# A four-layer graph network on one core: where neighbour rows are summed, and who adds the bias, the residual and the row sums

## The chip, the cores and the metric

The kernel runs on one core of a Trainium2 chip. That core has a matrix engine (PE, with its weight loads listed as PEld), a vector engine (DVE), a scalar engine (ACT), a general engine (POOL), a queue engine that issues plain transfers (SP), and 16 DMA engines. The engines run side by side, each takes its own instructions strictly in order, and they wait for one another through semaphores. The metric is the device time of one execution in microseconds (us): the median of three runs before the change is 1075.28 us (1071.92 to 1076.54).

## The reference, cut to what matters

There are 3327 nodes with 512 features each, and an adjacency matrix of 3327 x 3327 that is nearly empty (a node has about four neighbours). Four layers follow one another, all of the form x = x + layer(relu(layernorm(x))):

```
layer 0:  relu( self + (sum of neighbours' rows) / degree + bias )   self and neighbour weights folded beforehand
layer 1:  8 heads; softmax over the neighbours of leaky_relu(src + dst); weighted sum of the neighbours' rows
layer 2:  4 heads, the same, then elu
layer 3:  1 head, the same; weighted sum of the normalised inputs, then one 512 x 512 product with W
```

Every layer needs, for each node, the rows of its neighbours as the layer before left them. So no layer may gather a row before that row has been written.

## The kernel before, in words

**Preparation.** The kernel reads the whole adjacency matrix, and DVE finds the columns that hold a one. It makes a list of at most 16 neighbours per node (16 is `SLOTS`), sorts the nodes by falling degree, and cuts the sorted nodes into 26 chunks of 128. After the sort, slot s of a chunk is needed only by the nodes that have more than s neighbours. `ROWS` says how many sorted nodes may have a slot s; `CAPS` is the same in chunks, and `slots_of` turns it round: chunk 0 has 14 slots, chunk 1 has 8, chunks 2 and 3 have 7, chunks 4 to 6 have 6, 7 to 10 have 5, 11 to 15 have 4, 16 to 20 have 3, 21 to 23 have 2, 24 and 25 have 1. That is 117 slots in all. Alongside, PE multiplies the normalised input with the two folded weights of layer 0. The neighbour part goes to a table in DRAM. The own part is copied by ACT (`keep_y`, L1373) beside the input row, and POOL scatters both, with the list of neighbours, to the node's sorted place (`scatter`, L1435, one indirect transfer per chunk, 26 in all). One transfer (`back`, L1451) then brings the lists of all sorted nodes back into on-chip memory (`srec`), and DVE takes the reciprocal degrees from it (`degrees`, L1505 and L1506).

**The layers.** A layer goes through its chunks in units of one or two, in the order that `ORDERS` lists. For each slot of a chunk POOL issues one indirect transfer (`gather`, L1562) that brings 128 rows, or fewer where `held` says that fewer are needed, into one place of a ring of 33 places. A place is written again only when its readers are done. In layer 0 DVE notes the neighbours' sorted places (L1862), PE adds the first slots into PSUM by products with the identity matrix (`sum_on_pe`, L1593), DVE divides by the degree and adds the own part (L1871), adds the bias (L1879), adds the last `ON_DVE` slots one by one (L1887), and takes the relu and adds the input (L1895). In layers 1 and 2 DVE makes the scores and weights of a unit (L1941 to L1978), multiplies the rows in the ring by the weights (L2110; the first `ON_ACT` slots on ACT, L2096, one instruction per head), PE sums the slots, and in layer 1 DVE adds some of them (L2138). Then the result is added to the running x (L2148, L2172 and L2178). In layer 3 ACT and DVE weigh and add the rows (L2028, L2030), PE turns the sum (L2046), multiplies the residual by the identity (L2058) and the sum by W (L2060) into the same PSUM place, ACT copies it out (L2067), and POOL scatters it to the node's original row of the output (L2072).

**From one layer to the next.** `project` takes the mean and variance of the new rows on DVE (`bn_stats`, L1649 and L1650), guesses the reciprocal root on ACT (L822, L824) and refines it on DVE in four small operations per unit (L831 to L836), normalises on ACT (L1676), turns on PE (L1694), copies on ACT with column sums (L1705), multiplies by the next layer's weights on PE (L1780, eight products per chunk), copies on ACT (L1803 to L1806) and stores the rows to the next layer's table through SP (L1822). A switch `SUMMED` would take the mean from a row sum that the update leaves behind and the variance from a square on ACT; it is off for all layers. A layer's first gather waits for all stores of the layer before; a memset on POOL (`mark`, L2194) carries that wait.

**What sets the order.** `Plan` is a list scheduler that runs while the kernel is built. Each piece of work is given an engine, a cost in us and the pieces it follows; the plan replays them and emits the instructions in the order it finds. So the instruction order on every engine comes from the plan's costs, and at run time the engines keep to it.

Of the kernel before, what the change touches and what calls it, by code (L numbers as in the profile page):

```python
# [13 lines left out]
ALU = mybir.AluOpType  # L14
# [4 lines left out]
P = 128  # L19
# [7 lines left out]
def general_path(  # L27
# [519 lines left out]
    def l3_finish(pc, i, o):  # L547
# [16 lines left out]
ROWS = (3328, 3072, 2592, 1984, 1344, 832, 448, 224, 128, 64, 32, 32, 32, 32, 0, 0)  # L564
# [8 lines left out]
    0: {S: min(S // 2, 5) for S in range(1, SLOTS + 1)},  # L573
    1: {S: min(S // 2, 5) for S in range(1, SLOTS + 1)},
    2: {S: 0 for S in range(1, SLOTS + 1)},
# [4 lines left out]
        (24,), (12, 21), (11,), (6,), (18,), (17,), (15,), (4,), (3,), (20,), (5, 9), (22,), (10, 19), (1,),  # L580
        (2,), (14,), (0,), (23,), (8,), (13, 16), (7,), (25,),
    ),
    1: (
        (18, 21), (22, 24), (15,), (5,), (10, 20), (2,), (17,), (12, 23), (19,), (4,), (9, 14), (7,), (11, 16),
        (8, 13), (6,), (1,), (0,), (3,), (25,),
    ),
    2: (
        (18, 23), (19, 24), (16,), (20,), (6, 11), (10, 14), (7, 12), (5, 13), (9,), (1,), (21, 22), (4,), (0,),
        (8,), (2,), (3,), (15,), (17,), (25,),
    ),  # L590
    3: (
        (0,), (7,), (17,), (15, 20), (25,), (11,), (3,), (23,), (1, 5), (24,), (4, 14), (16,), (12, 22), (8,),
        (9,), (10,), (18,), (2,), (13,), (19,), (21,), (6,),
# [4 lines left out]
    1: {S: min(S // 3, 1) for S in range(1, SLOTS + 1)},  # L598
    2: {S: S // 5 for S in range(1, SLOTS + 1)},
}  # L600

SUMMED = {1: False, 2: False, 3: False}
# [90 lines left out]
def gnn_stack_kernel(  # L693
# [41 lines left out]
    with ExitStack() as st:  # L735
# [116 lines left out]
        with tc.tile_pool(name="p0", bufs=1) as pa, tc.tile_pool(name="p0p", bufs=2, space=PSUM) as pp:  # L852
# [444 lines left out]
            for p0 in range(0, NK, 2):  # L1297
# [25 lines left out]
                for j, i in enumerate(unit):  # L1323
# [51 lines left out]
                    own_done[i] = put("act", 0.62, late_rank, keep_y, (), [y], give=("py",))  # L1375
# [74 lines left out]
            def back():  # L1450
                ins = nc.sync.dma_start(srec_f, own.rearrange("(k p) w -> p k w", p=P)[:, :, 2 * D :])  # L1451
                for other in scattered:
                    tc.add_manual_dep(
                        ins.ins,
                        other.ins.name,
                        mybir.DependencyInfo(mybir.DependencyClass.Sync, mybir.DependencyReason.DATA),
                        reason="every row is read",
                    )
# [57 lines left out]
        with tc.tile_pool(name="run", bufs=1, reuse_waits="tile") as pr, tc.tile_pool(  # L1516
# [28 lines left out]
            def gather(layer, i, rank, barrier):  # L1545
# [8 lines left out]
                for s in range(S):  # L1554
# [16 lines left out]
                    landed.append(plan.add("dma", 0.95 * held(i, s) / P, rank, None, [issue], lag=1.3))  # L1571
                return ring[:, r0 : r0 + S, :], landed, last

            def runs_of(i, lo, hi, most=SLOTS):
# [7 lines left out]
                return out  # L1582

# [262 lines left out]
            for number, unit in enumerate(ORDERS[0]):  # L1846
                rank = (0, number)
                updated = []
                for j, i in enumerate(unit):
# [15 lines left out]
                    left = S - ON_DVE[0][S]  # L1865
                    summed = sum_on_pe(key, g, list(range(left)), [[o] for o in landed], rank)
# [9 lines left out]

                    def emit(key=key):
                        acc = tiles["acc", key]
                        nc.vector.tensor_tensor(acc, acc, biasf, ALU.add)  # L1879

                    done = plan.add("dve", 0.7, rank, emit, [done])
                    for s in range(left, S):

                        def emit(i=i, key=key, g=g, s=s):
                            m = held(i, s)
                            acc = tiles["acc", key][:m, :]
                            nc.vector.scalar_tensor_tensor(  # L1887
                                acc, g[:m, s, :D], rdeg[:m, i : i + 1], acc, ALU.mult, ALU.add
                            )

                        done = plan.add("dve", 0.7, rank, emit, [done, landed[s]])
                        last.append(done)
# [18 lines left out]
            def attend(layer, number, unit, barrier):  # L1911
# [80 lines left out]
                for j, i in enumerate(unit):  # L1992
# [56 lines left out]
                    if layer == 3:  # L2049
# [16 lines left out]
                        def emit(key=key):  # L2066
                            nc.scalar.copy(new("t", key, [P, WIDE])[:, :D], tiles["pw", key][:, 0, :])  # L2067
# [192 lines left out]
```

## Time and profile before

| what | value |
|---|---|
| three runs | 1071.92, 1075.28, 1076.54 us |
| profiled execution: span from the first to the last instruction | 1230.0 us (the page gives no other time of this execution) |
| busy time over the span: PE, DVE, ACT, POOL | 901.8, 726.6, 518.2, 610.1 us |
| preparation, up to the first gather | 0 to 278 us |
| layer 0, 1, 2, 3 | 278 to 514, 514 to 759, 759 to 998, 998 to 1230 us |
| mean granted clock of TensorE | 0.855 |

The profiled execution is 154.7 us longer than the median run, or 1.144 times. So a sum made on the profile is about the profiled execution, and has to be carried over to the runs. The stage borders are read from the `mark` memsets on POOL (514.21, 759.46 and 998.45 us) and from the first gather (278.18 us). Busy time per stage is more useful here than the total, because each layer waits for the one before it: a layer is as long as its most loaded engine needs, plus the time in which that engine has nothing to do at the start and at the end. "Idle before" in the groups of instructions is the waiting time of an engine just before such an instruction, and costs nothing where that engine is not the bottleneck.

### The profile page before, as it was taken

What the parts mean: (1) busy time and instruction counts of PE and PEld (TensorE: products, weight loads), DVE (VectorE), ACT (ScalarE), POOL (GpSimd) and SP (SyncE); (2) the same over time, 40 slices, a digit from 0 to 9 for tenths busy, and PEclk for the clock granted to TensorE, in tenths of its full rate; (3) what the DMA queues carried; (4) which work ended last, traced back from release to release, by engine and by line L of the source; (5) the groups of instructions that cost most, each with busy time, mean ns of one, the idle gap of its engine ahead of it and who ended that gap; (6) DMA issues with size and microseconds to landing.
All of it is one profiled execution on the core that took longest, in us unless ns stands there. A gap on an engine that the chain in (4) does not pass through costs nothing. (4 is left out here: it accounts for less than half of the span.)

```text
span 1230.0 us, 11605 instructions
## 1 busy us (share of the span) xinstructions
PE 901.8 (73%) x2853; PEld 510.4 (41%) x2853; DVE 726.6 (59%) x1848; ACT 518.2 (42%) x1700; POOL 610.1 (50%) x719
## 2 busy tenths in 40 slices
PE   7599999854098889752979796539979832948865
PEld 4244444322075656531647464214435421423322
DVE  6499989204176557453869784628894815534441
ACT  4488886210043433422656553316554621312221
POOL 1064246717655550175757511766883236675661
PEclk9899999977599899966989889659896956978987
DMA  9999894958587772265666521665754345575561
GB/s 352 338 364 338 294 306 146 317 203 286 172 268 252 247 249 89 76 195 149 198 183 178 154 79 55 189 187 150 209 169 129 91 121 149 168 206 160 163 186 59
DMA packets 89910, 240.49 MB, mean 196 GB/s; under 512 B 24933, under 2 KB 26477, under 8 KB 89834
## 3 DMA queue, kind: packets, MB, share of 16 engines
q0 software_dynamic: 41600, 137.72, 38.1%
q1 hardware_dynamic: 48234, 101.96, 23.3%
q8 instruction: 24, 0.39, 0.1%
q14 instruction: 52, 0.43, 0.1%
HBM read 190.35 MB, written 49.27 MB: 195 GB/s over the span
## 5 line engine op out<-in xcount | busy, mean ns | idle before, releaser
L1562 POOL DMA_INDIRECT ring<-table,nbr x351 | 368.5, 1050 | 185.5 <-issue 80.9
L1593 PE MATMUL acc<-ring,ident 128*128 128x512 f32 (+1 forms) x494 | 266.6, 676 | 66.8 <-DVE ring L2110 24.3
L1780 PE MATMUL pw<-w,hT 128*128 128x264 f32 (+1 forms) x832 | 197.3, 394 | 18.3 <-ACT hT L1705 13.6
L1780 PEld LDWEIGHTS pw<-w,hT 128*128 128x128 f32 x832 | 161.2, 195 | 60.9 <-ACT hT L1705 20.5
L1593 PEld LDWEIGHTS acc<-ring,ident 128*128 128x128 f32 (+1 forms) x494 | 98.7, 215 | 175.1 <-issue 107.5
L1562 POOL DMA_INDIRECT ring<-table,srec x117 | 110.1, 941 | 77.8 <-issue 31.5
L2110 DVE TENSOR_TENSOR ring<-ring,w 128x2048 f32<-128x2048 f32 (+7 forms) x76 | 114.3, 1531 | 4.7 <-DVE w L1978 3.0
L2060 PE MATMUL pw<-w,hT 128*128 128x512 f32 x208 | 101.7, 634 | 13.3 <-ACT hT L2052 11.0
L1209 DVE FIND_INDEX8 fidx<-one_i,ai 128x8 uint32<-128x832 int32 x104 | 104.2, 1018 | 0.0
L1349 PE MATMUL pz_n<-wf,hT_n 128*128 128x512 f32 x208 | 95.2, 609 | 10.9 <-ACT hT_n L1342 8.4
L1705 ACT ACTIVATE hT<-pt 128x128 f32<-128x128 f32 (+1 forms) x312 | 81.8, 292 | 39.7 <-PE pt L1694 18.5
L1217 ACT ACTIVATE junk<-ai 128x1664 int8<-128x1664 int32 (+1 forms) x52 | 82.7, 1590 | 32.6 <-DMA ai<-in_adj_dram 32.2
L1694 PE MATMUL pt<-ident,h 128*128 128x128 f32 x208 | 36.5, 312 | 75.9 <-ACT h L1676 73.4
L1349 PE MATMUL py_n<-wf,hT_n 128*128 128x512 f32 x208 | 91.9, 592 | 0.0
L1803 ACT COPY t<-pw 128x512 f32<-128x512 f32 (+1 forms) x54 | 30.6, 566 | 134.0 <-PE pw L1780 43.9
L1941 DVE TENSOR_TENSOR e<-ring,fs 128x24 f32<-128x24 f32 (+25 forms) x96 | 15.2, 172 | 120.2 <-DMA ring<-table,nbr 102.0
L2060 PEld LDWEIGHTS pw<-w,hT 128*128 128x128 f32 x208 | 42.3, 207 | 73.2 <-issue 51.3
L1705 ACT ACTIVATION_READ_ACCUMULATOR hT<-pt 128x1 f32 x312 | 69.5, 223 | 0.0
L1694 PEld LDWEIGHTS pt<-ident,h 128*128 128x128 f32 x208 | 28.1, 160 | 96.3 <-ACT h L1676 81.6
L2194 POOL MEMSET mark<- 1x1 f32 x3 | 0.3, 88 | 132.7 <-DMA table<-t 132.7
L1349 PEld LDWEIGHTS pz_n<-wf,hT_n 128*128 128x128 f32 x208 | 39.8, 195 | 62.8 <-issue 49.4
L2046 PE MATMUL pt<-ident,y 128*128 128x128 f32 x96 | 16.4, 312 | 67.4 <-issue 56.8
(185 smaller groups left out, 1319.7 us busy)
## 6 DMA issues: line engine op xcount, KB each, us to landing
ai<-in_adj_dram SPq DMA_DIRECT2D x25, 832.0 KB
ai<-in_adj_dram SPq DMA_DIRECT2D x25, 831.5 KB
table<-t SPq DMA_DIRECT2D x52, 258.0 KB
xy<-own SPq DMA_DIRECT2D x26, 512.0 KB
table<-t SPq DMA_DIRECT2D x26, 260.0 KB
table<-zt_n SPq DMA_DIRECT2D x26, 256.0 KB
ring<-table,nbr POOLq DMA_INDIRECT x351
later<-in_x_dram SPq DMA_DIRECT2D x15, 256.0 KB
```

The source lines that it names most:

```text
L1209: nc.vector.max_index(fidx[:, i, qq * 8 : (qq + 1) * 8], one_i, ai[:, q * QW : min(cols, (q + 1) * QW)])
L1217: nc.scalar.activation(junk[:, :cols], tiles["ai", key][:, :cols], AF.Square, accum_out=sq[:, i, hf : hf + 1])
L1349: nc.tensor.matmul(pz, tiles["hT", key][:, c, :], wf[s][:, c, :], start=(c == 0), stop=(c == DC - 1))
L1562: nc.gpsimd.indirect_dma_start(out=ring[:m, r0 + s, : width[layer]], out_offset=None, in_=table[layer], in_offset=bass.IndirectOffsetOnAxi ...
L1593: nc.tensor.matmul(acc, ident[:m, :], g[:m, s, :D], start=(k == 0), stop=(k == len(slots) - 1))
L1694: nc.tensor.transpose(pt[:, c, :], h[:, c * P : (c + 1) * P], ident)
L1705: nc.scalar.activation(hT[:, c, :n], pt[:, c, :n], AF.Copy, accum_out=hsum[layer][:, i, c : c + 1])
L1780: nc.tensor.matmul(pw[:, b, :w], tiles["hT", key][:, c, :], wsb[layer][:, c, b, :w], start=(c == 0), stop=(c == DC - 1),)
L1803: nc.scalar.copy(t[:, :D].rearrange("p (b f) -> p b f", b=2)[:, lo:hi, :], pw[:, lo:hi, :HD])
L2046: nc.tensor.transpose(pt[:, c, :], tiles["y", key][:, c * P : (c + 1) * P], ident)
L2060: nc.tensor.matmul(pw[:, 0, :], tiles["hT", key][:, c, :], w3[:, c, :], start=False, stop=(c == DC - 1))
L2110: nc.vector.tensor_tensor(v, v, box["w"][:m, j, lo:hi, :].unsqueeze(3).to_broadcast([m, hi - lo, H, O]), ALU.mult,)
```

## The change

- Gathers always bring whole slots of 128 rows: `ROWS` is rounded up to multiples of 128. The number of slots stays 117.
- In layers 0, 1 and 2 a chunk's slots are summed either all on PE or all on DVE, by one `tensor_reduce` that reads the slots of a feature one after another (a step of 520 words in the ring) and then goes to the next feature. `ON_DVE` now lists the chunks: 18 in layer 0 (82 slots), 11 in layer 1 (65 slots), 2 in layer 2 (9 slots). The one-by-one additions on DVE are gone.
- The bias of layer 0 is added on POOL in the preparation, chunk by chunk, right after `keep_y`; DVE's addition in layer 0 is gone.
- `back` brings the lists in 26 transfers, one per chunk in layer 0's order, in place of one.
- `ON_ACT` is given per chunk: 15 slots in layer 1 (21 before), 33 in layer 2 (12 before).
- `SUMMED` is on for layer 2: the update of layer 1 leaves row sums, and ACT squares.
- In layer 3 DVE adds the residual while it reads the product; PE's identity product and ACT's copy are gone.
- Other orders in all four layers (19, 17, 17 and 21 units, in place of 22, 19, 19 and 22), and the ring starts at its first place in each layer.

```diff
-ROWS = (3328, 3072, 2592, 1984, 1344, 832, 448, 224, 128, 64, 32, 32, 32, 32, 0, 0)
+ROWS = (3328, 3072, 2688, 2048, 1408, 896, 512, 256, 128, 128, 128, 128, 128, 128, 0, 0)
 ON_DVE = {
-    0: {S: min(S // 2, 5) for S in range(1, SLOTS + 1)},
-    1: {S: min(S // 2, 5) for S in range(1, SLOTS + 1)},
-    2: {S: 0 for S in range(1, SLOTS + 1)},
+    0: frozenset((0, 2, 4, 5, 7, 9, 10, 11, 12, 13, 15, 17, 18, 19, 20, 21, 22, 23,)),
+    1: frozenset((0, 1, 3, 4, 5, 7, 8, 9, 12, 19, 22,)),
+    2: frozenset((2, 22,)),
 }
 ORDERS = {
     0: (
-        (24,), (12, 21), (11,), (6,), (18,), (17,), (15,), (4,), (3,), (20,), (5, 9), (22,), (10, 19), (1,),
-        (2,), (14,), (0,), (23,), (8,), (13, 16), (7,), (25,),
+        (22,), (24, 14), (13,), (17, 19), (23,), (18, 20), (3,), (15,), (21, 16), (8,), (12,), (2,), (11, 10),
+        (0, 5), (1,), (4, 7), (6,), (9,), (25,),
...
     1: (
-        (18, 21), (22, 24), (15,), (5,), (10, 20), (2,), (17,), (12, 23), (19,), (4,), (9, 14), (7,), (11, 16),
-        (8, 13), (6,), (1,), (0,), (3,), (25,),
+        (24,), (22,), (10,), (21, 20), (19,), (5, 17), (16,), (12,), (15, 7), (2, 3), (13, 9), (6, 14),
+        (4, 11), (23, 8), (1, 18), (0,), (25,),
...
     2: (
-        (18, 23), (19, 24), (16,), (20,), (6, 11), (10, 14), (7, 12), (5, 13), (9,), (1,), (21, 22), (4,), (0,),
-        (8,), (2,), (3,), (15,), (17,), (25,),
+        (24, 22), (16,), (23, 18), (19, 8), (13, 17), (21, 15), (4,), (12, 6), (10, 7), (1,), (14, 20),
+        (11, 9), (5,), (3,), (0,), (2,), (25,),
...
     3: (
-        (0,), (7,), (17,), (15, 20), (25,), (11,), (3,), (23,), (1, 5), (24,), (4, 14), (16,), (12, 22), (8,),
-        (9,), (10,), (18,), (2,), (13,), (19,), (21,), (6,),
+        (2,), (7, 4), (14,), (6, 12), (0,), (1, 3), (22,), (23,), (13,), (5,), (10,), (18, 21), (8,), (24,),
+        (9,), (11,), (25, 15), (19,), (16,), (17,), (20,),
...
 ON_ACT = {
-    1: {S: min(S // 3, 1) for S in range(1, SLOTS + 1)},
-    2: {S: S // 5 for S in range(1, SLOTS + 1)},
+    1: (1, 2, 1, 0, 2, 1, 2, 1, 0, 1, 0, 0, 0, 0, 0, 0, 1, 1, 1, 0, 0, 1, 0, 0, 0, 0),
+    2: (5, 3, 2, 2, 2, 1, 1, 3, 0, 0, 2, 3, 1, 2, 0, 1, 2, 1, 0, 1, 0, 0, 0, 1, 0, 0),
 }
-SUMMED = {1: False, 2: False, 3: False}
+SUMMED = {1: False, 2: True, 3: False}
...
-                    own_done[i] = put("act", 0.62, late_rank, keep_y, (), [y], give=("py",))
+                    o = put("act", 0.62, late_rank, keep_y, (), [y], give=("py",))
+                    def add_bias(i=i):
+                        own = node(i)[:, D : 2 * D]
+                        nc.gpsimd.tensor_tensor(own, own, biasf, ALU.add)
+                    own_done[i] = put("pool", 1.28, late_rank, add_bias, (), [o, whole])
...
-                ins = nc.sync.dma_start(srec_f, own.rearrange("(k p) w -> p k w", p=P)[:, :, 2 * D :])
+                for k in (k for unit in ORDERS[0] for k in unit):
+                    ins = nc.sync.dma_start(srec_f[:, k, :], own[k * P : (k + 1) * P, 2 * D :])
...
+            def sum_on_dve(key, g, S, needs, rank):
+                def emit():
+                    nc.vector.tensor_reduce(
+                        new("acc", key, [P, D], pp), g[:, :S, :D].rearrange("p s d -> p d s"), AX.X, ALU.add
+                    )
+                return [plan.add("dve", 0.1 + 0.535 * S, rank, emit, needs, take=("acc",))]
...
-                            nc.tensor.matmul(pw[:, 0, :], ident, xres[:, i, :], start=True, stop=False)
...
-                            nc.scalar.copy(new("t", key, [P, WIDE])[:, :D], tiles["pw", key][:, 0, :])
+                            nc.vector.tensor_tensor(
+                                new("t", key, [P, WIDE])[:, :D], tiles["pw", key][:, 0, :], xres[:, i, :], ALU.add
+                            )
```

## The prediction

> **What bounds the kernel now.** I read the busy times by stage first, because a layer cannot gather before the layer before it has stored, so each stage has a bound of its own.
>
> ```profile
> core 0: us, PE busy (x) PEld busy (x) DVE busy (x) ACT busy (x) POOL busy (x), PEclk, DMA share, GB/s
> 0.00:278.00 278.00, 234.03 (x639) 110.37 (x639) 187.22 (x520) 163.33 (x263) 104.95 (x222) 0.95 0.83 295
> 278.00:514.00 236.00, 173.87 (x651) 118.85 (x652) 130.56 (x305) 77.36 (x353) 110.13 (x117) 0.88 0.65 209
> 514.00:759.00 245.00, 180.97 (x652) 121.84 (x651) 165.93 (x397) 119.27 (x539) 124.02 (x118) 0.85 0.51 149
> 759.00:998.00 239.00, 172.54 (x550) 93.81 (x548) 151.47 (x374) 110.60 (x449) 134.12 (x118) 0.78 0.52 153
> 998.00:1230.00 232.00, 140.40 (x364) 65.50 (x364) 91.37 (x252) 47.59 (x96) 136.86 (x144) 0.79 0.53 156
> ```
>
> PE is the most loaded engine in layers 0, 1 and 2, with DVE 15 us behind in layer 1. PE's time without work is 62.1, 64.0 and 66.5 us there. In layer 3 POOL leads: an issue lasts 0.95 us with 0.30 us between, so 143 issues take 179 of its 232 us.
>
> The waits say where a stage loses time:
>
> ```profile
> POOL mark L2194 <- DMA table<-t: 132.7, 3, 56.1
> ...
> POOL out_dram L2072 <- ACT t L2067: 37.1, 10, 5.9
> ```
>
> POOL ends its gathers long before a layer ends (132.7 us over three borders), so layers 0 to 2 are not set by the gathers but by the work that lags behind them. In layer 3 POOL itself waits for finished outputs. Next, the groups of instructions that the edits touch, shapes apart:
>
> ```profile
> L1593 PE MATMUL acc<-ring,ident 128*128 128x512 f32 x472 | 254.0, 675 | 66.7 <-DVE ring L2110 24.3 <-issue 22.6 <-DMA ring<-table,srec 15.3
> ...
> L1649 DVE BATCH_NORM_STATS2 st<-xres 128x6 f32<-128x512 f32 x78 | 53.7, 689 | 2.0
> ...
> L1887 DVE SCALAR_TENSOR_TENSOR acc<-ring,rdeg,acc 128x512 f32<-128x512 f32 x39 | 29.4, 755 | 1.2
> ...
> L2138 DVE TENSOR_TENSOR acc<-ring,acc 128x512 f32<-128x512 f32 x39 | 27.0, 693 | 18.5 <-PE acc L1593 17.0 <-issue 0.9
> ...
> L1879 DVE TENSOR_TENSOR acc<-acc,biasf 128x512 f32<-128x512 f32 x26 | 18.1, 698 | 0.7
> ```
>
> and DVE's reductions that exist already, which price the new one:
>
> ```profile
> L1245 DVE TENSOR_REDUCE deg<-low 128x2 f32<-128x64 f32 x2 | 0.4, 210 | 0.0
> L1245 DVE TENSOR_REDUCE deg<-low 128x6 f32<-128x192 f32 x3 | 1.0, 345 | 0.0
> L1423 DVE TENSOR_REDUCE rank<-ai_sort 128x26 f32<-128x416 f32 x1 | 1.0, 951 | 0.0
> L1717 DVE TENSOR_REDUCE tot<-hsum 128x4 f32<-128x100 f32 x3 | 1.0, 333 | 8.5 <-ACT hT L1705 8.5
> ```
>
> L1245 reads neighbouring words: (345 - 210) / 128 = 1.05 ns a word and 0.14 us fixed. L1423 steps 26 words, L1717 4 words: (951 - 143) / 416 = 1.94 and (333 - 143) / 100 = 1.90 ns.
>
> **The price of a sum on DVE.** The new sum steps 520 words. Its bounds are the contiguous rate (0.54 us a slot of 512) and, above, 2.1 ns, the steepest strided row (L1950, 128x28 in 202 ns): 1.08 us. I take 1.9 ns, from the two longest strided rows: 0.97 us a slot, 0.14 us per sum. The plan's cost is 0.535 us a slot, so DVE will run behind its plan.
> [...]
>
> **Preparation, +3.3 us.** POOL gets 26 bias additions. The nearest row is POOL's 128x512 product at L1131, 1278 ns, so 33 us; POOL is busy 105 of 278 us, and that idle time hides all but the end. The last copy of an own part (L1373) ends at 268.46 us. Before, one scatter follows and ends at 270.16. In the changed order the last addition waits for that copy and three scatters stand behind it: 268.6 + 1.3 + 3 x 1.25 - 0.3 = 273.4. Were the idle time not there, the cost would be 33 us.
>
> **Lists in 26 transfers, +4 us.**
>
> ```profile
> 273.23 0.37 SPq L1451 DMA_DIRECT2D srec<-own  x1
> ```
> ```profile
> 277.38 0.18 DVE L1505 CAST degs<-srec 128x26 f32<-128x26 int32 x1 [9.06 <-DMA srec<-own]
> 277.60 0.32 DVE L1506 RECIPROCAL rdeg<-degs 128x26 f32<-128x26 f32 x1
> ...
> 284.84 0.76 DVE L1871 SCALAR_TENSOR_TENSOR acc<-acc,rdeg,xy 128x512 f32<-128x512 f32 x1 [1.98 <-PE acc L1593]
> ```
>
> The first gather now waits for the first list only, which can win it about 2 us. But DVE's cast reads all lists and stands first in its queue, and the loads of own rows stand behind the 26 issues on SP. Two neighbouring issues on SP took 0.81 us, so the last goes out 10 us after the first and lands, as the one before did, 3.8 us later. With the cast, the reciprocal and the first sum (2.1 us), the first L1871 comes 17.0 us after the first issue, against 11.6: 5.4 us late. Lower bound -2 (the gathers lead), upper 5.4; I take 4, since DVE will lead layer 0.
>
> **Layer 0, -10 us.** DVE loses 50 additions (37.6) and the bias (18.1), and gains 82 x 0.97 + 18 x 0.14 = 82.4. Three units and eight short casts fewer save 3.1. So 130.6 becomes 154.2. PE loses 32 of 67 slots at 66.0 / 67: 173.9 becomes 142.4. DVE takes over. With PE's 62 us without work, and 10 us more at the end (behind DVE's last row still come ACT 0.8, PE 0.6, ACT 2.0, PE 3.7, ACT 0.9 and a store): 154.2 + 62 + 10 = 226 against 236. At 0.54 us a slot DVE has 119 and PE leads: 142 + 62 = 204, -32. At 1.08, -1.
>
> **Layer 1, -1 us.** DVE: 165.9 - 34.6 (additions) - 22.6 (statistics, 26 x 0.871) + 64.8 (65 slots, 11 sums) + 3.2 (six slots back from ACT, 0.54 each) + 2.6 (centring, one 0.16 us operation a unit) + 1.5 (row sums; no row shows one: 0 to 3) - 5 (fewer units, no ragged pieces) = 175.8. PE: 181.0 - 15 x 1.12 = 164.2. ACT: 119.3 - 6 x 2.02 + 26 x 1.04 = 134. DVE leads: 175.8 + 64 + 10, less 6 because DVE has its first scores 6 us ahead of PE's first sum: 244 against 245. Bounds -17 (PE leads at 0.54) and +7.
>
> **Layer 2, -4 us.** PE loses 9 slots at 1.11: -10. ACT takes 21 more slots at 1.28 us: 110.6 becomes 137.5 of 239, in the same queue as the copies that free PE's PSUM places. DVE falls to 146. ACT's 27 us cost nothing if PE never waits; I charge a quarter, 6. Bounds -10 and +17.
>
> **Layer 3, -3 us.** PE loses 31.2, ACT 15.2, DVE gains 26 x 0.69 = 18; none leads. POOL's 37 us of waits for outputs shrink by one product (0.86) on 10 outputs, -9 at best; but the new addition stands behind weighted sums of 0.75 us each on DVE: eight of these in front of outputs give +6. Bounds -9 and +6. The first unit has 7 slots in place of 14, but POOL is issuing then anyway.
>
> Whole slots add 832 rows a layer (6%) to transfers; DMA is busy 0.5 to 0.65 in the layers, which hides them. 1.0 would be needed for a cost.
>
> Sum: 3.3 + 4 - 10 - 1 - 4 - 3 = -10.7 us on a profiled span of 1230.0, or 0.9913. The runs' median is 0.874 of that span, and nothing shows which waits the profile adds, so I scale: 1075.28 x 0.9913 = **1066 us**.
>
> **Rivals.**
> - *Slower: the sums hold DVE's queue.* The 29 sums of layers 0 and 1 last 5 us on average, 13.8 us for 14 slots; behind each stand the refinements (L831 to L836) of an earlier unit, for which ACT, and then PE, wait. If a third of each sum becomes idle time on PE that nothing fills, it costs 49 us in the profile, 43 in runs: 1108. It decides from 0.6 us per sum. For it: the plan's cost is near half of mine, and layer 1 ends on chunk 0 with 14 slots. Against: other chunks' products lie ready on PE.
> - *Sums at the contiguous rate.* PE leads in layers 0 and 1: -32 and -17, in all -49: 1033. Against: both strided rows.
> - *No change.* Layer 0 has a stretch of 36 us near 297 to 333 in which PE and DVE stand still because ACT does; if such stretches take the 10 us back, 1075.
>
> **How the numbers follow.** About 0.5% is what a measurement here tells from no change (1070 to 1081 is the same). My forecast has 0.40 (own range 1050 to 1080: 0.33 faster, 0.05 same, 0.02 slower), the slower rival 0.35 (0.33 slower), contiguous sums 0.12, no change 0.13 (0.09 same). That is faster 0.47, same 0.16, slower 0.37. The range goes from 1030, below the cheap sums, to 1108, at the slower rival's price: about 0.05 below, 0.12 above.
>
> **What would show it.** Sums at 0.97 us a slot (7 slots 6.9 us); DVE near 154 and 176 us busy in layers 0 and 1, PE near 142 and 164; last scatter 3 us later; layer 0's own-part operation 17 us after the first list issue; `mark` waits no longer than before. The prediction is wrong if a slot costs 0.6 or 1.2 us, if DVE's share in layer 0 stays under 0.6 while PE's falls, or if ACT's waits grow in layer 2.

## The result and the profile after

The changed kernel takes 1114.84 us (median of four runs, 1112.09 to 1117.66) against 1075.91 us (four runs, 1071.92 to 1077.20): 1.036 of the kernel before, 95% interval 1.0328 to 1.0393. It is 3.6% slower; 1066 us were forecast, with a range of 1030 to 1108. A second set of four runs gave 1.0328 (1.0288 to 1.0367).

In some sets of runs the kernel before takes 1076 us and in others, on other chips, 1200 to 1240 us, and the profiled execution that the prediction worked from (1230.0 us) is of the second kind; stages are compared below only where the kernel before takes 1076 us.

There the kernel before was profiled again. These are the busy times by stage, cut at the first gather of each layer, first of the kernel before (run `r1_before`), then of the changed kernel in the same set (run `r2_after`). After the window's length come the busy times of PE, PEld, DVE, ACT and POOL, then the granted clock of TensorE, the share of the DMA engines and GB/s.

```profile
core 0: us, PE busy (x) PEld busy (x) DVE busy (x) ACT busy (x) POOL busy (x), PEclk, DMA share, GB/s
0.00:268.47 268.47, 232.13 (x639) 109.79 (x639) 186.57 (x520) 163.09 (x263) 104.97 (x223) 0.96 0.87 306
268.47:451.94 183.47, 167.62 (x654) 114.79 (x654) 130.72 (x305) 78.36 (x359) 110.30 (x119) 0.97 0.81 270
451.94:657.66 205.72, 171.28 (x650) 117.91 (x650) 165.07 (x397) 118.85 (x539) 129.17 (x119) 0.92 0.63 177
657.66:871.40 213.74, 172.06 (x546) 93.22 (x546) 150.73 (x374) 110.17 (x443) 140.12 (x118) 0.80 0.60 170
871.40:1075.70 204.30, 132.75 (x364) 62.22 (x364) 91.63 (x252) 47.25 (x96) 136.78 (x143) 0.83 0.61 177
```
```profile
0.00:272.75 272.75, 234.29 (x639) 110.42 (x639) 194.95 (x518) 163.06 (x263) 136.06 (x248) 0.95 0.84 299
272.75:472.88 200.13, 153.12 (x590) 109.63 (x590) 143.49 (x229) 76.66 (x353) 110.78 (x118) 0.88 0.76 259
472.88:689.75 216.87, 166.15 (x620) 119.53 (x620) 170.41 (x306) 126.81 (x536) 134.03 (x118) 0.88 0.62 176
689.75:895.64 205.89, 156.03 (x528) 88.29 (x528) 143.31 (x337) 132.44 (x521) 128.64 (x119) 0.80 0.64 184
895.64:1109.70 214.06, 123.88 (x312) 55.98 (x312) 106.48 (x265) 34.77 (x70) 137.48 (x143) 0.79 0.62 177
```

The preparation is 4.3 us longer, layer 0 16.7, layer 1 11.2 and layer 3 9.8; layer 2 is 7.9 us shorter. Together that is the 34 us between the two spans. The reader should look at PE's busy time against the length of layer 0: before, 167.6 of 183.5 us, so PE stood idle for only 15.9 us, not for the 62 that the prediction carried along. After, PE has 14.5 us less to do and idles for 47.0. In layer 1 the idle time goes from 34.4 to 50.7, while 5.1 us of work went away.

The profile of the changed kernel that came with its first result (span 1115.8 us) has the same stages: 200.1, 216.6, 205.6 and 218.1 us. The waits that answer to those shown of before, and one that grew:

```profile
POOL mark L2188 <- DMA table<-t: 119.6, 3, 43.3
PE pt L1710 <- ACT h L1692: 62.1, 15, 12.4
POOL out_dram L2074 <- DVE t L2067: 13.8, 7, 3.8
```

and the groups, shapes apart (count, then busy time and ns of one):

```profile
L1609 PE MATMUL acc<-ring,ident 128*128 128x512 f32 x382 | 200.9, 666 | 64.9 <-DMA ring<-table,nbr 20.0 <-DMA ring<-table,srec 18.5 <-DVE xres L1896 10.9
L1665 DVE BATCH_NORM_STATS2 st<-xres 128x6 f32<-128x512 f32 x52 | 35.7, 687 | 1.2
L1594 DVE TENSOR_REDUCE acc<-ring 128x512 f32<-128x2560 f32 x6 | 28.5, 4754 | 0.1
L1594 DVE TENSOR_REDUCE acc<-ring 128x512 f32<-128x7168 f32 x2 | 26.2, 13106 | 0.1
...
L1594 DVE TENSOR_REDUCE acc<-ring 128x512 f32<-128x1536 f32 x5 | 9.6, 1912 | 0.0
...
L1594 DVE TENSOR_REDUCE acc<-ring 128x512 f32<-128x1024 f32 x5 | 6.2, 1238 | 0.1
```

A sum of 5 slots takes 4.75 us and one of 14 slots 13.1: 0.94 to 0.95 us a slot. PE's waits for `h`, the normalised rows, come to 62.1 us; in the kernel before (`r1_before`) they were 9.9. POOL's waits at `mark`, which the prediction expected to be no longer than before, are 119.6 us, against 105.3 in `r1_before`. How a sum makes PE wait for `h` is seen in one place of layer 0. This is the time line of the changed kernel (`r2_after`) at the unit of chunks 4 and 7 (start, duration, engine, line; in brackets the idle time and what ended it):

```profile
432.33 0.18 DVE L1666 BATCH_NORM_AGGREGATE mv<-st 128x2 f32<-128x6 f32 x1
432.35 4.46 PE L1609 MATMUL acc<-ring,ident 128*128 128x512 f32 x10
...
432.61 4.73 DVE L1594 TENSOR_REDUCE acc<-ring 128x512 f32<-128x2560 f32 x1
...
437.37 0.76 DVE L1889 SCALAR_TENSOR_TENSOR acc<-acc,rdeg,xy 128x512 f32<-128x512 f32 x1
...
439.62 0.18 DVE L1666 BATCH_NORM_AGGREGATE mv<-st 128x2 f32<-128x6 f32 x1
439.84 0.30 ACT L822 ACTIVATE ln<-mv,eps 128x2 f32<-128x2 f32 x1 [6.56 <-DVE mv L1666]
...
441.28 1.52 ACT L1692 ACTIVATE h<-xres,nmr,rs 128x512 f32<-128x512 f32 x2 [0.81 <-DVE nmr L836]
...
442.14 0.69 PE L1710 MATMUL pt<-ident,h 128*128 128x128 f32 x2 [5.33 <-ACT h L1692]
```

Chunk 4 has its statistics at 432.5. The sum of chunk 7 then holds DVE until 437.3, its division, relu and statistics until 439.8. ACT has nothing for 6.6 us, then guesses the root for both; DVE refines it; and PE, which finished its products at 436.8, gets `h` at 442.1. DVE is busy without a break from 432.3 to 439.8 us, although over the whole layer it is busy for only 143.5 of 200.1 us; ACT and then PE wait behind it.

### The profile page after: what moved, and what is told of

The parts are those of the page before. It is cut to its first block, busy times and chain, and to the rows that moved or that the text cites. A ratio compares the mean times of both kernels' runs of the same rounds, so it can differ in the third digit from the quotient of the medians.

```text
span 1115.8 us, 10987 instructions
## 1 busy us (share of the span) xinstructions
PE 833.5 (75%) x2689; PEld 484.5 (43%) x2689; DVE 760.1 (68%) x1655; ACT 533.2 (48%) x1743; POOL 647.5 (58%) x745
## 5 line engine op out<-in xcount | busy, mean ns | idle before, releaser
L1569 POOL DMA_INDIRECT ring<-table,nbr x351 | 374.9, 1068 | 120.4 <-issue 77.1
L1609 PE MATMUL acc<-ring,ident 128*128 128x512 f32 x382 | 200.9, 666 | 64.9 <-DMA ring<-table,nbr 20.0
L1796 PE MATMUL pw<-w,hT 128*128 128x264 f32 (+1 forms) x832 | 205.2, 407 | 12.1 <-ACT hT L1721 12.1
L1796 PEld LDWEIGHTS pw<-w,hT 128*128 128x128 f32 x832 | 167.3, 203 | 52.3 <-ACT hT L1721 18.8
L1594 DVE TENSOR_REDUCE acc<-ring 128x512 f32<-128x2560 f32 (+7 forms) x31 | 138.7, 4473 | 2.8 <-ACT t L1771 2.5
L1609 PEld LDWEIGHTS acc<-ring,ident 128*128 128x128 f32 x382 | 76.0, 213 | 143.3 <-issue 61.9
L2060 PE MATMUL pw<-w,hT 128*128 128x512 f32 x208 | 109.9, 681 | 14.5 <-ACT hT L2053 14.5
L2112 DVE TENSOR_TENSOR ring<-ring,w 128x2048 f32<-128x2048 f32 (+3 forms) x66 | 105.5, 1624 | 1.5
L1217 ACT ACTIVATE junk<-ai 128x1664 int8<-128x1664 int32 (+1 forms) x52 | 82.7, 1591 | 37.0 <-DMA ai<-in_adj_dram 36.6
L1710 PE MATMUL pt<-ident,h 128*128 128x128 f32 x208 | 36.9, 320 | 62.2 <-ACT h L1692 62.1
L2098 ACT ACTIVATE ring<-ring,w 128x128 f32<-128x128 f32 (+1 forms) x252 | 71.3, 376 | 6.7 <-DVE w L1979 5.8
L2060 PEld LDWEIGHTS pw<-w,hT 128*128 128x128 f32 x208 | 43.4, 218 | 68.6 <-issue 47.8
L2188 POOL MEMSET mark<- 1x1 f32 x3 | 0.3, 88 | 119.6 <-DMA table<-t 119.6
L2047 PE MATMUL pt<-ident,y 128*128 128x128 f32 x96 | 16.7, 306 | 65.8 <-DVE y L2031 62.8
L1969 ACT ACTIVATE ex<-el 128x24 f32<-128x24 f32 (+19 forms) x51 | 11.7, 229 | 107.4 <-DVE el L1952 107.4
```

The costliest lines, as they stand in the source:

```text
L1217: nc.scalar.activation(junk[:, :cols], tiles["ai", key][:, :cols], AF.Square, accum_out=sq[:, i, hf : hf + 1])
L1569: nc.gpsimd.indirect_dma_start(out=ring[:m, r0 + s, : width[layer]], out_offset=None, in_=table[layer], in_offset=bass.IndirectOffsetOnAxi ...
L1594: nc.vector.tensor_reduce(new("acc", key, [P, D], pp), g[:, :S, :D].rearrange("p s d -> p d s"), AX.X, ALU.add)
L1609: nc.tensor.matmul(acc, ident[:m, :], g[:m, s, :D], start=(k == 0), stop=(k == len(slots) - 1))
L1710: nc.tensor.transpose(pt[:, c, :], h[:, c * P : (c + 1) * P], ident)
L1796: nc.tensor.matmul(pw[:, b, :w], tiles["hT", key][:, c, :], wsb[layer][:, c, b, :w], start=(c == 0), stop=(c == DC - 1),)
```

## The experiments

Stage times in us between first gathers, from one profile each; the ratio is that of the timed runs. Two profiles of the changed kernel differ by 0.3 us or less in layers 0 to 2, by 2.6 in the preparation and by 4.1 in layer 3; two other kernels with the same layer 3 (`q1_halves` and `t1_halves_bn`) differ by 6.8 there. A single number here can bear no more than that. The expectations of `r1_before`, `e7_residual_pe` and `b1_layer2` have some of these stages cut at the `mark` memsets in place of the first gathers, or rounded.

| run | preparation | layer 0 | layer 1 | layer 2 | layer 3 | ratio to the kernel before |
|---|---|---|---|---|---|---|
| `r1_before` | 268.5 | 183.5 | 205.7 | 213.7 | 204.3 | 1 |
| `r2_after` | 272.8 | 200.1 | 216.9 | 205.9 | 214.1 | 1.0328 (1.0288 to 1.0367) |
| `p2_whole_slots` | 268.9 | 183.2 | 215.6 | 209.1 | 210.5 | 1.0121 (1.0086 to 1.0155) |
| `p1_sums` | 268.3 | 206.4 | 238.2 | 224.2 | 211.6 | 1.0698 (1.0659 to 1.0736) |
| `t2_sums_halves` | 268.3 | 194.2 | 218.1 | 220.8 | 212.6 | 1.0366 (1.0333 to 1.0399) |
| `q1_halves` | 272.6 | 184.4 | 219.0 | 203.1 | 219.7 | 1.0191 (1.0155 to 1.0227) |
| `t1_halves_bn` | 272.7 | 184.7 | 227.5 | 202.2 | 212.9 | 1.0254 (1.0226 to 1.0282) |
| `e9_true_cost` | 272.4 | 193.1 | 237.1 | 201.6 | 212.8 | 1.0412 (1.0377 to 1.0447) |
| `e7_residual_pe` | 271.5 | 200.0 | 217.3 | 205.3 | 210.5 | 1.0326 (1.0276 to 1.0375) |
| `b1_layer2` | 266.4 | 183.5 | 207.5 | 208.1 | 205.7 | 0.9969 (0.9945 to 0.9993) |

**Both kernels again, as the measure.** Neither kernel is changed.

> The kernel before once more. Its first two profiled executions (1230 and 1198 us) were both far above the 1075 us of its other runs; in both, PE, DVE and ACT stand still together some 125 us of the span, 23.8 us of it near 300 us. If this run is near 1075 us, its split by stage can be set against the changed kernel's (275, 196, 217, 203, 225 us): the loss of 39 us should then show as layers 0 and 1 near 185 and 200 us (theory B, the sums), or as layers 2 and 3 near 185 and 205 us (theory C).

> The changed kernel again, as the measure for the runs that undo one part of it. Every theory expects a ratio of 1.036 to the kernel before if the loss has nothing to do with the surroundings of the run; a ratio off by more than 1% says that it has.

Measured 1077.75 and 1111.58 us. The loss lies in layers 0, 1 and 3, so neither theory B nor C has it alone.

**The sums' rule and the whole slots, each added to the kernel before.** `p2_whole_slots` changes only `ROWS`. `p1_sums` adds to it (layer 0 shown, shortened; layers 1 and 2 alike):

```diff
+if i in ON_DVE[layer]: summed = sum_on_dve(key, g, S, landed, rank)    # the changed kernel's lists
+else:                  summed = sum_on_pe(key, g, list(range(S)), ...)
-left = S - ON_DVE[layer][S]        # PE sums these; DVE adds the other slots one by one
```

> The kernel before with whole slots alone (832 rows more a layer). Prediction: nothing, 0.995 to 1.005, because transfers are hidden. If the added rows cost what they move (1.66 KB by 4.3 MB a layer at 190 GB/s, 9 us a layer): up to 1.02 to 1.03. Fewer short operations on DVE (casts, products and scores by piece) could give 0.5% back.

> The kernel before with the changed kernel's rule for sums alone: whole chunks on DVE where the lists say so, all others on PE, and the whole slots that this needs; orders, bias, lists, layer 2's statistics, ACT's slots and layer 3's residual as before. Theory B (the sums hold DVE's queue): slower, 1.03 to 1.06 of the kernel before. Prediction's working (DVE leads layer 0 at 154 us in place of PE at 174): no slower than 1.00 in layer 0, 1.00 to 1.02 in all. Theory A (the orders): 1.00 to 1.01.

(In the first of these the price of the rows is garbled; 832 rows of 2.08 KB are 1.7 MB, by estimate about 10 us at the 177 GB/s that layers 1 and 3 of `r1_before` show.) Whole slots cost 1.2%, so they are not free: 9.9 us in layer 1 and 6.2 in layer 3, with 4.6 gained in layer 2. The traces have PE's operations in the same order as before in layers 2 and 3, but in another order in layers 0 and 1, since the plan's costs change with `ROWS`; what layer 1 shows is both together. The sums' rule costs 61.5 us more in the profile (1148.7 against 1087.2), more than any theory expected: 23 us each in layers 0 and 1, and 15 in layer 2, where only two chunks are summed on DVE. In these three layers the plan also made another order of ACT's and PE's work, so this is the price of the rule with the order that follows from it. Layers 0 and 1 of the two, first whole slots alone, then with the sums:

```profile
268.88:452.08 183.20, 167.19 (x654) 114.60 (x654) 130.57 (x297) 78.61 (x359) 110.99 (x119) 0.98 0.83 280
452.08:667.65 215.57, 171.49 (x650) 117.14 (x650) 164.22 (x378) 119.58 (x539) 132.10 (x119) 0.91 0.62 177
```
```profile
268.29:474.71 206.42, 156.92 (x590) 112.09 (x590) 162.70 (x265) 78.22 (x359) 110.95 (x118) 0.87 0.74 248
474.71:712.91 238.20, 165.66 (x620) 117.04 (x620) 189.67 (x339) 120.05 (x539) 128.51 (x118) 0.86 0.56 160
```

PE lost 64 matmul records of layer 0 but only 10.3 us of busy time, and its clock went from 0.98 to 0.87. DVE got 32 us more. Neither fills the 206 us.

**Is it the price of a sum, or that it is on DVE?** `q1_halves` is the changed kernel with the same plan and order, but neighbouring words are added: the 31 sums take 78.7 us in place of 138.6. `t2_sums_halves` is `p1_sums` with the same edit, and also keeps its order. So these two pairs differ in the form of the sums alone.

```diff
-nc.vector.tensor_reduce(new("acc", ...), g[:, :S, :D].rearrange("p s d -> p d s"), AX.X, ALU.add)
+m = S
+while m > 2:
+    h = m // 2
+    nc.vector.tensor_tensor(g[:, :h, :D], g[:, :h, :D], g[:, m - h : m, :D], ALU.add)
+    m -= h
+nc.vector.tensor_tensor(new("acc", ...), g[:, 0, :D], g[:, 1, :D], ALU.add)
```

> The changed kernel, same chunks, same plan and order, but a DVE sum is made of additions of neighbouring words: the upper half of the slots is added onto the lower half until two are left, and these go to PSUM (7 slots: 3 + 2 + 1 in place of one strided reduction). By the product's row (0.535 us a slot) 7 slots cost about 3.6 us in place of 6.6, and the 31 sums about 80 us in place of 138. Theory B (the length of the sums holds DVE's queue, and PE waits behind it): layers 0 and 1 get back most of what they lost, 1.00 or less of the kernel before. Theory F (a sum on DVE costs its latency in any form, because it starts only when all slots have landed): 1.02 or more. The prediction's rival of sums at the contiguous rate said 49 us less than before in a profile of 1230 us.

> Once more the kernel before with whole slots and the changed kernel's rule for sums, the sums by halves. Strided: 1.070, and 206 and 238 us in layers 0 and 1; whole slots alone: 1.012, and 183 and 216 us. If length is the whole cost of the rule: 1.00 to 1.015, layers 0 and 1 near 183 and 216. If half is that a sum waits for all slots: 1.035 to 1.045, layers 0 and 1 near 195 and 227.

In the changed kernel the cheap sums took layer 0 from 200.1 to 184.4 us, as long as before; layer 1 did not move (216.9 and 219.0), though DVE has 25 us less to do there:

```profile
272.61:457.00 184.39, 148.07 (x590) 105.11 (x590) 113.14 (x252) 76.17 (x353) 124.16 (x119) 0.92 0.82 281
457.00:676.02 219.02, 165.98 (x620) 119.92 (x620) 145.16 (x325) 126.80 (x536) 143.44 (x118) 0.88 0.61 174
```

On the kernel before, cheap sums leave 26.8 of the rule's 61.5 us (1114.0 against 1087.2). In layer 0 of `t2_sums_halves` DVE has hardly more work than with whole slots alone (132.7 and 130.6 us) and PE has 14.5 less, and still the layer is 11 us longer; PE waits 22.6 us for `h`, against 3.1. So a little over half of the rule's cost is the strided form. The rest, 11 us each in layers 0 and 2, comes with whole sums on DVE and with the order that the plan makes around them; these two were not separated. The theory of length alone falls for the rule as such, and it holds for layer 0 of the changed kernel. With 1.0191 in all, `q1_halves` lies between what the two theories expected.

**Was the order made with a wrong price?**

```diff
-return [plan.add("dve", 0.1 + 0.535 * S, rank, emit, needs, take=("acc",))]
+return [plan.add("dve", 0.1 + (0.62 if S < 4 else 0.93) * S, rank, emit, needs, take=("acc",))]
```

> The changed kernel, where the plan that orders the instructions is told the measured price of a sum (0.62 us a slot up to three slots, 0.93 above) in place of 0.535; nothing else changes but the order of instructions. If the loss is that the order was made for sums of half their length: 1.02 or less. If it is the length itself: 1.03 to 1.04, as the changed kernel.

1.0412: no gain. Layer 0 is 7 us shorter and layer 1 20 us longer. The order is not made worse by the wrong price in sum.

**Layer 3's residual back on PE** (shortened).

```diff
+nc.tensor.matmul(pw[:, 0, :], ident, xres[:, i, :], start=True, stop=False)
...
-nc.vector.tensor_tensor(new("t", key, [P, WIDE])[:, :D], tiles["pw", key][:, 0, :], xres[:, i, :], ALU.add)
+nc.scalar.copy(new("t", key, [P, WIDE])[:, :D], tiles["pw", key][:, 0, :])
```

> The changed kernel with layer 3's residual on PE and its copy on ACT again. Layer 3 of the changed kernel takes 220 us against 205. If the addition's place in DVE's queue is the cause: layer 3 10 us shorter or more, 1.02. If the order of layer 3 is: no change, 1.03; PE's 26 more products of 0.66 us can make it 1.035.

Layer 3 is 3.6 us shorter in the profile, and the runs do not tell it from the changed kernel. It then takes 210.5 us, like the three kernels with whole slots and the old layer 3 (210.5, 211.6 and 212.6); without whole slots it was 204.3 and 205.7. So of layer 3's 9.8 us, about 6 go with the whole slots, and the rest, no larger than the scatter of that stage, with the residual and the order together.

**Layer 2's parts on the kernel before.** `ORDERS[2]` and `ON_ACT[2]` of the changed kernel.

> The kernel before with two parts of the changed kernel, both in layer 2: its order of units and its share of slots on ACT (33 in place of 12). Layer 2 is the only one that became shorter, 217 to 204 us. If these two parts did it: 0.985 to 0.99. If it was the row sums that layer 1 leaves for it, or the whole slots: 0.998 to 1.005. Prediction's step (ACT's slots hold up PE's PSUM places): up to 1.01.

Layer 2 takes 208.1 us against 213.7, with ACT busy 132.9 in place of 110.2. In the runs the gain is 0.3%, where 1 to 1.5% were expected if these parts did it all. This kernel is the only one of the study whose interval lies below 1. Whole slots alone shortened layer 2 too, by 4.6 us, so the changed kernel's 7.9 us are not divided between the two here.

**What keeps layer 1 long.** With sums by halves, `t1_halves_bn` sets `SUMMED[2]` to False.

> Once more the changed kernel with sums by halves and layer 2's mean and variance by DVE's statistics. Where the kernel before takes 1076 us, the sums by halves alone had 219 us in layer 1 and 1.019. Theory E (row sums): layer 1 near 208 us, 1.01. Theory G (whole slots, which alone had 216 us in layer 1): 215 to 220, 1.015 to 1.02.

Layer 1 became longer, 227.5 us: with the row sums, and the order that goes with them, it is 8.5 us shorter, and theory E falls. Theory G's 215 to 220 did not come either. PE's waits in layer 1, of the kernel before and of the changed one (us in total, times, longest):

```profile
PE acc L1593 <- DVE ring L2110: 22.6, 4, 16.0
PE pt L1694 <- ACT h L1676: 6.3, 5, 2.4
```
```profile
PE pt L1710 <- ACT h L1692: 43.7, 9, 12.4
```

With sums by halves the wait for `h` is 45.3 us, and 54.4 with the statistics too. The longest, 12.4 us, is at the start of the layer, where the new order has a chunk of one slot and nothing that PE could sum. But before, PE waits there too, 16.0 us for its first product and then 4.9 more. The loss is at the other end. These are the first 140 us of the layer and the rest, before and after:

```profile
451.94:591.94 140.00, 113.40 (x425) 77.53 (x426) 116.89 (x291) 84.50 (x382) 109.82 (x100) 0.90 0.76 213
591.94:657.66 65.72, 57.88 (x226) 40.38 (x225) 48.18 (x107) 34.35 (x158) 19.35 (x20) 0.97 0.35 101
```
```profile
472.88:612.88 140.00, 114.35 (x408) 78.09 (x408) 111.60 (x226) 84.78 (x353) 110.75 (x97) 0.89 0.75 208
612.88:689.75 76.87, 51.80 (x212) 41.44 (x212) 58.81 (x81) 42.03 (x183) 23.28 (x22) 0.84 0.38 118
```

After 140 us PE has done as much as before; in the rest it waits for `h` three times, 21.1 us in all, against 2.7. So the start is not the cause, and the length of the sums alone is not either, since cheap sums leave the layer as long as it was. What else in the new order, and in the whole slots, holds up `h` was not separated; the cause of layer 1's loss stays open.

**Runs in sets where the kernel before takes 1226 and 1235 us.** Their ratios hold within their own set only.

> The kernel before, unchanged, profiled a second time, because its first profiled execution was 155 us longer than its runs. Every theory expects a time within 1070 to 1081 us; the use is the split by stage, against the changed kernel's 275, 196, 217, 203 and 225 us (preparation, layers 0 to 3). If the sums of layers 0 and 1 are the loss, these two layers are together at least 25 us shorter here than 413 us; if the residual addition or the order of layer 3 is the loss, layer 3 is at least 20 us shorter than 225; if the row sums or the larger share of ACT in layer 2 are, layer 2 is at least 20 us shorter than 203.

1199.94 us, where every theory had 1070 to 1081. By the time lines PE, DVE and ACT stood idle together, in stretches of over 2.5 us after the first 240 us, for 127 us in all, against 61 in `r1_before`.

`e2_old_orders` puts `ORDERS` of before into the changed kernel, `e3_pe_sums` empties `ON_DVE`, `e4_bn_layer2` sets `SUMMED[2]` to False:

> The changed kernel with the four orders of units of the kernel before, all else as changed. Theory A (the orders are the loss): 1085 us or less, most of the 39 us returned. Theory B (the sums hold DVE's queue, the orders were chosen for them): 1115 us or more, since the old orders put chunk pairs and long sums elsewhere. Theory C (layer 3 alone is the loss, by its order): about 1095.

> The changed kernel with every chunk summed on PE, none by a DVE sum. Theory B (the sums hold DVE's queue): PE gains 156 slots of about 1.1 us, 172 us over three layers, of which the idle time of PE hides a part; DVE loses 139 us; the end comes 20 us or more earlier, 1095 or less. Theory A (the orders): no gain, PE leads layers 0 and 1 by more, 1125 to 1150. Theory D (the sums pay, as the prediction had it, and the loss is in other parts): 1125 to 1150 as well; the split by stage tells A from D only together with the run of the old orders.

> The changed kernel with layer 2's mean and variance by DVE's statistics again (26 of 0.69 us and 26 aggregations come back on DVE, 26 squares of 1.04 us leave ACT). Theory E (the row sums and squares on ACT lengthen each unit's chain in the second half of layer 1): 5 to 15 us less than the changed kernel, 1100 to 1110. Prediction's working (DVE leads layer 1): layer 1 longer by up to the 17 us of DVE's work that returns, 1115 to 1130.

1.0552 (1.0449 to 1.0655), 1.0456 (1.0359 to 1.0552) and 1.0364 (1.0260 to 1.0469). Each of the three is slower than the kernel before in its own set. The changed kernel itself was not run there, so they do not say what each part gives back: neither whether the new orders are better than the old ones (theory A stays open), nor what sums on PE alone would bring. The latter is in any case no return to the kernel before, which shares the slots of each chunk between PE and DVE.

The other set held `s1_halves_bn` (the kernel of `t1_halves_bn`), `s2_halves_order1` (sums by halves and the old order of layer 1), `p3_sums_halves` (the kernel of `t2_sums_halves`) and `e6_one_list` (the changed kernel with the lists in one transfer):

> The changed kernel with sums by halves (as before) and layer 2's mean and variance by DVE's statistics again. With sums by halves alone the stages by first gathers were 273, 184, 219, 203 and 220 us. Theory E (the row sums and squares are what keeps layer 1 long): layer 1 10 us shorter, near 208, 1.01 of the kernel before. Theory A (layer 1's order): layer 1 stays at 219 or, with 17 us more on DVE, rises to 225.

> The changed kernel with sums by halves and layer 1 in the order of the kernel before. Theory A (the new order of layer 1, which starts with chunks of 1, 2 and 5 slots and leaves PE without work at the start): layer 1 near 208 in place of 219. Theory E (row sums): layer 1 stays at 215 or more. Theory G (neither: whole slots, which alone cost layer 1 10 us on the kernel before): 215 or more here and in the run with the statistics.

> The kernel before with whole slots and the changed kernel's rule for sums, the sums by halves. With strided sums this was 1.070, with whole slots alone 1.012. If length is the whole cost of the rule: 1.00 to 1.015. If half the cost is that a sum on DVE starts only when all slots have landed and been weighed: 1.035 to 1.045.

> The changed kernel with one transfer for all lists in place of 26. Prediction: 4 us shorter in layer 0 (its first own-part operation 11.6 us after the first issue in place of 18), with at most 2 us later first gather; 1.03. If the layer's gathers lead and the late start is hidden: no change, 1.033 to 1.036, or 2 us longer.

1.0017 (0.9976 to 1.0058), 1.0064 (1.0026 to 1.0102), 0.9958 (0.9913 to 1.0003) and 1.0047 (1.0006 to 1.0088). The first and third are the same kernels that gave 1.0254 and 1.0366 above. So the totals of these two sets say nothing for the place where the forecast is judged. Two local readings still stand: one list brings the first own-part operation 12.0 us after the list's issue (269.86 to 281.89) in place of 17.9 (270.31 to 288.18); and layer 1's order stays open, since `s2_halves_order1` (252 us) and `s1_halves_bn` (238) are no further apart than two profiles of the kernel before in such sets (245 and 230).

## Why the prediction was wrong, point by point

**The step that failed** is layer 0's: "With PE's 62 us without work, and 10 us more at the end [...]: 154.2 + 62 + 10 = 226 against 236." It has two faults. The 62 us were of an execution of 1230 us, and 36.6 of them were a single wait for `h`, the stretch from 299 to 336 us that the prediction names under its third rival. Where the runs take 1076, PE idles for 15.9 us in that layer (12.1 if it is cut at the `mark`, as the prediction cut it). The scaling at the end of the sum (0.874) could not repair that, since it shrinks work and idle time alike. The second fault is worse: idle time was taken as a constant that any change of work leaves alone. With the right 15.9 and the measured busy times the same rule gives 153 + 16 + 10 = 179 us, again a gain; 200.1 was measured, with 47.0 us of idle time on PE. PE's waits in layer 0, before, after, and with sums by halves:

```profile
PE acc L1593 <- DMA ring<-table,srec: 18.7, 4, 17.3
PE pt L1694 <- ACT h L1676: 3.6, 4, 1.0
```
```profile
PE acc L1609 <- DMA ring<-table,srec: 20.0, 1, 20.0
PE pt L1710 <- ACT h L1692: 17.2, 7, 5.3
PE acc L1609 <- DVE xres L1896: 10.6, 2, 8.1
PE pw L1796 <- ACT hT L1721: 8.5, 9, 3.0
```
```profile
PE acc L1612 <- DVE xres L1899: 8.0, 1, 8.0
PE pt L1713 <- ACT h L1695: 3.4, 5, 1.3
```

The order is the same in the last two kernels, so what goes with the halves goes with the length of the sums. The wait for `h` does, from 17.2 to 3.4 us: it is the refinements that stand behind a sum. In all, the halves take 30.4 us off DVE in this layer, and it becomes 15.7 us shorter, by 10.7 us of PE's idle time and 5.1 of its busy time. That is nearly the whole 16.7 us of the loss. But even then the layer is only as long as before, though PE has 19.5 us less to do than there: its idle time is 36.3 us. The wait for `acc`, a place in PSUM, has another cause: 8.1 of its 10.6 us are one wait at the start of the layer, which stays with the halves. DVE cannot begin there before its cast has all 26 lists:

```profile
286.45 0.18 DVE L1512 CAST degs<-srec 128x26 f32<-128x26 int32 x1 [26.50 <-DMA srec<-own]
289.78 1.22 PE L1609 MATMUL acc<-ring,ident 128*128 128x512 f32 x1 [8.09 <-DVE xres L1896]
```

With the lists in one transfer (`e6_one_list`) PE waits only 0.3 us at this place, where `s1_halves_bn`, of the same set and with 26 transfers, waits 9.6. The waits for `hT` are 5.8 us with the halves; their cause is not shown.

**The price of a sum** was right where it was costly and wrong where it was cheap: 0.91 to 0.95 us a slot from four slots on (0.97 taken), but 0.62 and 0.64 for two and three, where the prediction itself had called 0.6 a sign of being wrong. In layers 0 and 1 the sums took 71.2 and 59.6 us against 82.4 and 64.8. "DVE takes over" did not happen: DVE is busy 143.5 of 200.1 us, PE 153.1. At 14 slots the row gives (13.106 - 0.14) / 7168 = 1.81 ns a word, near the 1.94 and 1.90 ns of the two strided rows that the prediction went by. At two slots it gives (1.238 - 0.14) / 1024 = 1.07 ns, hardly more than the 1.05 ns that L1245 takes for neighbouring words: there the extra cost is not seen. No row that the prediction had steps 520 words; that 1.9 ns would hold there, and for every length, was the author's estimate.

**PE's 31.5 us less in layer 0** (173.9 to 142.4) became 14.5, because what PE kept got slower. Groups of PE in layer 0, before and after:

```profile
L1780 PE MATMUL pw<-w,hT 128*128 128x264 f32 x414 | 95.6, 387 | 0.7 <-ACT hT L1705 0.7
L1593 PE MATMUL acc<-ring,ident 128*128 128x512 f32 x134 | 65.8, 619 | 20.5 <-DMA ring<-table,srec 18.7 <-DVE xres L1895 1.8
```
```profile
L1796 PE MATMUL pw<-w,hT 128*128 128x264 f32 x415 | 101.9, 405 | 8.5 <-ACT hT L1721 8.5
L1609 PE MATMUL acc<-ring,ident 128*128 128x512 f32 x70 | 39.1, 699 | 30.7 <-DMA ring<-table,srec 20.0 <-DVE xres L1896 10.6
```

The products of the same 26 chunks keep PE busy for 6.3 us longer, and the 70 matmuls that are left of the sums take 0.56 us of busy time each in place of 0.49, 4.7 us in all: 11 of the 17 us that are missing. The granted clock of the stage fell from 0.97 to 0.88. Before, it is at half for the first 9.7 us of the layer and then full. After, it is at half for the first 21.6 us, and again five times for 3.4 to 6.9 us, each time with or just after a wait of PE of 2.6 to 5.3 us. Two of these stretches:

```profile
272.75:294.30 21.55, 6.60 (x8) 2.44 (x9) 6.99 (x18) 1.40 (x3) 16.37 (x18) 0.50 0.88 270
441.00:447.90 6.90, 5.76 (x16) 4.10 (x17) 2.71 (x7) 4.20 (x20) 0.00 (x0) 0.51 0.23 78
```

The first profile of the changed kernel (`after`) has five such stretches too, of 3.4 to 6.9 us beside waits of 2.6 to 5.6 us; but a wait of 3.1 us there (390.1 to 393.3) leaves the clock at full, so what sets it back is not shown. What it costs is: an identity product of the sums lasts 0.96 us at half clock (409.1 to 412.2) and 0.63 at full (412.5 to 416.0), a product with the weights 0.66 (379.7 to 385.0) and 0.39 (385.5 to 389.6). The prediction had no term for this: PE lost time in the matmuls beside its waits too.

**The other terms.** Preparation: +3.3 forecast, +4.3 measured. The list transfers: the first own-part operation was forecast 17.0 us after the first issue and came after 17.9, and the first gather 2.5 us earlier; it made the 8.1 us wait shown above; what this costs at the layer's end was not measured apart. Layer 1: -1 forecast, +11.2; PE's work fell by 5.1 us and not by 16.8, and waits for `h` took the place of waits for products, the costly ones in the last third of the layer. Layer 2: -4 forecast, -7.9; the 6 us charged for ACT's copies did not come: in `b1_layer2` the layer is 5.7 us shorter, and PE's wait for the copies of `hT` is 1.4 us, against 2.3. Layer 3: -3 forecast, +9.8, of which about 6 are the whole slots. **Whole slots** were costed at nothing because DMA is busy only half the time; they cost 11.5 us of the profile. A DMA share below 1 did not hide them: layer 3, at a share of 0.61 before, is about 6 us longer in three kernels, with PE's order unchanged. What exactly runs later with them is not shown.

**The rivals.** The slower rival had the mechanism in layer 0: refinements behind a sum, then ACT, then PE. Its "third of each sum" is 10.7 / 30.4, or 0.35, there; in layer 1 the halves took 25.3 us off DVE and gave PE no idle time back. That its total, 1108, is near 1114.84 is in part luck: halves return 1.4%, some 15 us, where it charged 43, and the rest was lost in terms that it shared with the forecast. "Against: other chunks' products lie ready on PE" was the argument that kept it at 0.35; they did not cover the waits, since PE idled for 47.0 us in layer 0. The rival of contiguous sums, 1033, was wrong even with its price granted: 1096.10 us. So it had the same constant idle time and the same unpriced parts.

## What to carry to other kernels

Before costing a change as "work off the busiest engine", check that the profiled execution is as long as the runs, and read how much of the stage that engine really stands idle; idle time read from a longer execution is not slack: the 62 us of layer 0 were 15.9 where the runs take 1076. Moving a whole sum onto the engine whose short operations feed the others can cost a good part of its length wherever those operations stand behind it, however the totals of the engines balance: in layer 0 a third of what the sums were too long came back as idle time on PE. An operation that needs every part of a split transfer can start later than with one transfer: DVE's cast came 16.1 us after the first list's issue, against 4.1 in `r1_before`. And a slower clock beside longer waits of PE has to be priced too: in layer 0 it went from 0.97 to 0.88 while PE's idle time went from 15.9 to 47.0 us.

## What the runs showed of the hardware

The strided reduction showed two speeds (`after`): 1.07 and 1.15 ns a word for two and three slots, 1.7 to 1.8 ns from four on, at the same step of 520 words. Why the short sums are faster is not shown. And the ratio of two kernels is not a property of the kernels alone: the same pair gave 1.0366 where the kernel before takes 1076 us and 0.9958 where it takes 1235. In the second kind of set PE, DVE and ACT stand still together for twice as long (127 us in `e1_before_again`, 61 in `r1_before`). Why was not found; each set of the experiments ran on another chip, so the chip and the time of the run are not told apart.
